# Four graph layers on one core: bias additions on GpSimd, one spread load, and a schedule found anew

## The chip, the cores and the metric

The kernel runs on one core of a Trainium2 chip. A core has five engines that work side by side, each on its own list of instructions in its own fixed order: TensorE (PE, matrix products and transposes), VectorE (DVE), ScalarE (ACT), GpSimd (POOL) and SyncE (SP, which here only issues transfers). Transfers run on 16 DMA engines that all queues share. The metric is the device time of one execution in microseconds (us), lower is better. Before the change it is 3014.25 us, the median of three runs between 3012.17 and 3017.27.

## The reference

Thirty-two graphs of 512 nodes with 256 features each go through four layers. Each layer ends in `x = layernorm(x + layer(x))`. All data is float32.

```
layer 0:  h = (1+eps)*x + adj@x ;  relu(h@W1 + b1)@W2 + b2
layer 1:  h = x@W per head (4 heads) ; e = leaky_relu(e_dst[i] + e_src[j])
          masked where adj <= 0.5 ; softmax over j ; attn@h + bias
layer 2:  q,k,v of 8 heads ; softmax(q.k/sqrt(32) + log(adj + 1e-6)) @ v ; @Wo.T + bo
layer 3:  softmax(mask(((x@W) @ x.T) * adj)) @ x
```

Three of the layers add a bias row of 256 numbers to every node: `b2`, `bias` and `bo`.

## The kernel before, in words

A graph lies in SBUF as 128 partitions by four chunks of nodes. One graph is a few hundred steps, each with an engine, an estimated duration, the steps that it needs, and the buffers that it takes and frees. `graph(g)` (line 556) declares these steps for each of the 32 graphs, `prepare()` those that load and transpose weights. Nothing is emitted yet. `Plan.order` (line 135) then walks through all steps as a list scheduler: among the steps that could start within `ahead` of the earliest one it takes that with the earliest due time, and so writes the one order in which every engine will work. Steps of up to six graphs are interleaved in that order, so that while one graph is in layer 0 another is in layer 2 or 3. `Plan.run` at the end of `fast_path` is called with the period, the other parameters, and fourteen pairs of a random seed and a distance that shift due times: the result of a search by annealing. What the planner believes of durations and of landing times decides the order; on the chip each instruction simply waits, in that order, until what it needs is there.

The planner also keeps stocks of buffers: `B` (8 KB per partition, such as the attention weights of one head or one chunk), `C` (4 KB), `D` (2 KB strips), and `p`, the eight PSUM banks. A transfer is three steps: the issue on a queue's engine, a time on the modelled queue (`.q`), and a landing delay of 2.0 us, written in `transfer` (line 315).

The parts around the change:

- **Biases.** `prepare` copies each bias row four times into a DRAM tile `biases`. `bias_steps(k)` (line 577) adds it to all of `x` (128x1024) by a GpSimd-issued transfer that accumulates in SBUF (line 583), after the last PE step that still needs the unbiased `x`: the product `h` in layer 0, the transposes `xt1` and `xt2` in layers 1 and 2. The result `xb{k}` is needed by the residual addition on VectorE.
- **Row R of layer 1.** For each head, `R` is a row of 512 factors that must stand on every partition. It is made as a column tile (with two further columns `xs`, sums of features), transposed on PE (`Rt`, line 853), copied by VectorE (`Re`), stored to DRAM as 18 rows in one transfer (`Rs`, line 863), and loaded back spread over the partitions in four transfers, one per head, into four `D` strips (`Rl0` to `Rl3`, line 872). A fifth transfer spreads the two `xs` rows (`hsb`, line 880), which VectorE multiplies with weights (`hsl`, line 888).
- **What uses R.** Sixteen ScalarE steps `z{h}{c}` (line 911) apply a relu to the spread row; VectorE multiplies the edge mask in (`zm`, line 922); PE forms the sums (`o1`, line 946). ScalarE also copies every PSUM result of PE, among them `he0` and `he1` (line 731), which the product `f` (line 747) needs.
- **Forms of the PE array.** Most products use the whole array. Scores `s` (line 1116) use four groups of 32 rows at once, `n` and `d1`, `d2` (lines 1174, 994, 1204) four groups of 32 columns, `o1` two groups of 64 columns. Products of the four or two groups run together.

Of the kernel before, what the change touches and what calls it, by code (L numbers as in the profile page):

```python
# [30 lines left out]
def row_bcast(ap, n):  # L31

    return bass.AP(tensor=ap.tensor, offset=ap.offset, ap=[[0, P], [1, n]])
# [13 lines left out]
class Plan:  # L47
# [30 lines left out]
    def step(self, name, eng, us, after=(), take=(), free=(), mode=""):  # L78


        def add(emit):
            steps = self.steps[-1]
            known = {**steps, **{f"^{n}": s for n, s in self.steps[0].items()}}
            assert name not in steps and all(a in known for a in after), (name, after)
            takes = []
            for b in take:
                kind, _, key = b.partition("=")
                key, _, rest = key.partition("/")
                takes.append((kind, key or kind, int(rest or 0)))
# [135 lines left out]
def fast_path(  # L225
# [65 lines left out]

    wT = {n: const.tile([P, DC, D], F32, name=f"w{n}T") for n in ("q", "k", "v", "o")}
    w3_sb = const.tile([P, DC, D], F32, name="w3_sb")
    biases = dram.tile([3, NC, D], F32, tag="biases", name="biases", bufs=1)


    def blk(i):
# [1 line left out]


    plan = Plan({
        "B": 11, "C": 12, "D": 19, "p": 8,

        "live": 6, "L0": 1, "L1": 2, "L2": 2, "L3": 1, "AT": 4, "zs": 7, "edge": 1, "tmp": 2,
    })
# [2 lines left out]
    def prev(name, i):  # L308

        return (f"{name}{i-1}",) if i else ()  # L310

    def row(name, n):
        return tuple(f"{name}{i}" for i in range(n))

    def transfer(name, us, after, queue="q1"):


        @step(f"{name}.q", queue, us, after)
        def _():
            pass  # L320

        @step(name, None, 2.0, (f"{name}.q",))
        def _():
            pass


    def prepare():
# [10 lines left out]
        def load(name, us, *transfers, take=(), little=False):  # L338


            @step(f"ld_{name}", "act" if little else "sp", 0.5 * len(transfers), take=take)
            def _():
                for transfer in transfers:
                    (nc.scalar if little else nc.sync).dma_start(*transfer())

            transfer(name, us, (f"ld_{name}",), "q3" if little else "q1")

        def rows(w):
            return w.rearrange("(c p) f -> p c f", p=P)
# [34 lines left out]
        load("w1", 2.5, lambda: (w1_sb, rows(w1)))  # L384
        load("w2", 2.5, lambda: (w2_sb, rows(w2)))

        def bias_rows(k, b):

            return lambda: (
                biases[k : k + 1], bass.AP(b.tensor, b.offset, [[0, 1], [0, NC], [1, D]])  # L390
            )

        load("bias", 0.6, *(bias_rows(k, b) for k, b in enumerate((b2, gbias, bo))), little=True)

        def vector(name, a):
            def transfer():
# [159 lines left out]
    def graph(g):  # L556
# [11 lines left out]
        def strip(key, shape, name):  # L568
            return sb.tile(shape, F32, tag=f"D{slot[key]}", name=f"{name}_{g}")
# [7 lines left out]
        def bias_steps(k, after):  # L577


            @step(f"xd{k}", "pool", 0.95, after + ("^bias",))  # L580
            def _():
                line = biases[k - 1 : k].rearrange("o c d -> o (c d)")
                nc.gpsimd.dma_start(  # L583
                    t["x"].rearrange("p c d -> p (c d)"), row_bcast(line, NC * D), accum_op=ALU.add
                )

            @step(f"xq{k}", "qa", 3.0, (f"xd{k}",))
            def _():
                pass

            @step(f"xb{k}", None, 2.5, (f"xq{k}",))
            def _():
                pass

        def norm_stats(n, c):
            nc.vector.bn_stats(t[f"st{n}"][:, c, :], t["xo" if n == 4 else "x"][:, c, :])  # L596
# [61 lines left out]
        for c in range(NC):  # L658

            @step(  # L660
                f"la{c}i", "sp", 0.45, (f"la{c-1}i",) if c else (),
                take=(f"D=A0{c}/5",) if c else ("live", "L0", "D=A00/8"),
            )
            def _(c=c):
                t[f"A{c}"] = strip(f"A0{c}", [P, N], f"A{c}")
                nc.sync.dma_start(t[f"A{c}"], adj[g].rearrange("(c p) m -> p c m", p=P)[:, c, :])

            transfer(f"la{c}", 1.0 if g == 0 else 2.0, (f"la{c}i",))

        @step("lxi", "sp", 0.45, (f"la{NC-1}i",), take=("C=x/2",))  # L670
        def _():
# [187 lines left out]

        @step("Rsi", "sp", 0.45, ("Re",))  # L860
        def _():
            t["Rdram"] = dram.tile([H1 * NC + DC, P], F32, tag="R_dram", name=f"R_dram_{g}")
            nc.sync.dma_start(t["Rdram"], t["Rr"])

        transfer("Rs", 0.2, ("Rsi",))

        for h in range(H1):

            @step(f"Rl{h}i", "sp", 0.45, ("Rs",) + ((f"Rl{h-1}i",) if h else ()), take=(f"D=R{h}/4",))
            def _(h=h):  # L870
                t[f"R{h}"] = strip(f"R{h}", [P, N], f"R_bc_{h}")
                nc.sync.dma_start(t[f"R{h}"], row_bcast(t["Rdram"][h * NC : (h + 1) * NC, :], N))

            transfer(f"Rl{h}", 0.8, (f"Rl{h}i",))


        @step("hsbi", "sp", 0.45, ("Rs",), take=("D=xsr/3",))
        def _():
            t["xsr"] = strip("xsr", [P, 2, D], "xs_row")
            nc.sync.dma_start(t["xsr"][:, 0, :], row_bcast(t["Rdram"][H1 * NC :, :], D))  # L880

        transfer("hsb", 0.4, ("hsbi",))

        @step("hsl", "dve", 0.7, ("hsb", "^weg"), free=("xsr",))
        def _():
# [18 lines left out]
        for h in range(H1):  # L904
            for c in range(NC):

                @step(f"z{h}{c}", "act", 0.7, (f"Rl{h}", "ST") + prev(f"z{h}", c), take=() if c else (f"B=z{h}",))
                def _(h=h, c=c):
                    if c == 0:
                        t[f"e{h}"] = big(f"z{h}", [P, NC, N], f"z1_{h}")  # L910
                    nc.scalar.activation(  # L911
                        t[f"e{h}"][:, c, :], t[f"R{h}"], AF.Relu,
                        bias=t["nT"][:, h, c : c + 1], scale=t["S"][:, h, c : c + 1],
                    )
# [12 lines left out]
        for h in range(H1):  # L927
            plan.free(f"R{h}", row(f"z{h}", NC))


        for hp in range(H1 // 2):
# [484 lines left out]
    for g in range(B):  # L1416
        graph(g)
    with tc.manual_schedule():
        plan.run([(33, 0.0, 6, 55.0, ((619770, 10.0), (518002, 10.0), (122525, 2.0), (401816, 5.0), (736052, 5.0), (898543, 5.0), (151957, 2.0), (89616, 2.0), (541939, 5.0), (120127, 10.0), (238703, 2.0), (316405, 2.0), (831071, 5.0), (164665, 2.0)), (0.7, 0.0, 0.0))])

# [470 lines left out]
```

## Time and profile before

| | value |
|---|---|
| median of three runs | 3014.25 us |
| the profiled execution: its time / its span | 3010.3 us / 3008.2 us |
| PE busy | 2938.5 us (98%) |
| VectorE, ScalarE, GpSimd busy | 2060.2, 1928.2, 626.8 us |
| transfers `x<-biases` | 96 of 512 KB, issued by GpSimd, 5.5 us from issue to landing |
| transfers `R_bc<-R_dram` | 128 of 256 KB, issued by SyncE |
| transfers `xs_row<-R_dram` | 32 of 128 KB, issued by SyncE |
| VectorE idle until `xs_row` landed | 209.2 us in 28 waits |
| ScalarE idle until `R_bc` landed | 181.6 us in 37 waits |

The span goes from the first to the last instruction of one profiled execution; its time includes what lies around it. Busy time of PE is the union of modelled instruction intervals, each of which goes on past the start of the next one, so 98% does not say that PE streams data 98% of the time. The start of one matmul to the start of the next is the better measure. A wait is put down to the releaser that came last.

### The profile page before, as it was taken

The numbers are of one execution on the slowest core, as the hardware profiler recorded it, in microseconds if no ns is written. First come the engines' busy times: TensorE is split into PE (matmuls) and PEld (weight loads), VectorE is DVE, ScalarE is ACT, GpSimd is POOL, SyncE is SP. The second block draws the span as 40 slices with busy tenths as digits, with TensorE's granted clock in tenths as the row PEclk, the third lists the DMA queues.
The fourth block names the chain that finished last, engine by engine and source line by source line (L and its number), as shares of the span: only waits on it lengthen the run. The fifth ranks groups of instructions, "written<-read, shape, count | busy, mean of one in ns | idle before, by whom it ended". The sixth has DMA issues, their size and how long they took to land.

```text
span 3008.2 us, 42752 instructions
## 1 busy us (share of the span) xinstructions
PE 2938.5 (98%) x15521; PEld 1687.7 (56%) x15521; DVE 2060.2 (68%) x4133; ACT 1928.2 (64%) x3818; POOL 626.8 (21%) x688
## 2 busy tenths in 40 slices
PE   8999999999999999999999999999999999999998
PEld 6546565565555565655656556555556565565544
DVE  3567767667667677676676766766767767667776
ACT  4666766666666667566676666665666766657664
POOL 1222212222122221222211222212222212222120
PEclk9999999999999999999999999999999999999999
DMA  6887787787787787877878777778778787786770
GB/s 175 179 173 171 166 188 161 167 177 156 173 176 168 164 173 166 191 159 160 182 149 192 163 167 175 163 167 186 164 165 168 163 191 157 166 179 143 163 171 15
DMA packets 180320, 498.89 MB, mean 166 GB/s; under 512 B 17980, under 2 KB 57736, under 8 KB 156296
## 3 DMA queue, kind: packets, MB, share of 16 engines
q0 software_dynamic: 77472, 346.06, 60.4%
q1 hardware_dynamic: 101648, 149.75, 15.5%
q8 instruction: 125, 2.05, 0.3%
q14 instruction: 91, 0.75, 0.1%
q10 hardware_dynamic: 984, 0.28, 0.0%
HBM read 183.25 MB, written 17.08 MB: 67 GB/s over the span
## 4 chain that ended last, share of the span: by engine, by line
PE 73%; DVE 10%; DMA 9%; ACT 5%; issue 2%; POOL 1%; SPq 0%; ACTq 0%; POOLq 0%; DVEq 0%
PE s L1317 8%; PE o_ps L1174 7%; PE s L1116 7%; PE y_ps L766 7%; PE o_ps L946 6%; DVE z L922 5%; PE o_ps L1371 5%; PE iT_ps L1303 4%; PE h1T_ps L747 4%; PE v_ps L815 4%; PE o2p_ps L1259 4%; ACT z L911 4%; PE v_ps L1097 4%; DMA xs_row<-R_dram 3%; DMA R_bc<-R_dram 3%; PE qT_ps L1079 2%
## 5 line engine op out<-in xcount | busy, mean ns | idle before, releaser
L1138 DVE SCALAR_TENSOR_TENSOR z<-AT,z 128x1024 f32<-128x1024 f32 x512 | 616.3, 1219 | 214.4 <-ACT z L1129 210.2
L1129 ACT ACTIVATE z<-s 128x512 f32<-128x512 f32 x1024 | 566.1, 602 | 126.9 <-PE s L1116 123.0
L911 ACT ACTIVATE z<-R_bc,nT,S 128x512 f32<-128x512 f32 x512 | 380.0, 809 | 181.7 <-DMA R_bc<-R_dram 181.6
L637 ACT ACTIVATE x<-x,shift,rstd 128x256 f32<-128x256 f32 x508 | 283.2, 592 | 127.9 <-DVE shift L627 127.8
L922 DVE SCALAR_TENSOR_TENSOR z<-z,T,edge 128x512 f32<-128x512 f32 x512 | 350.4, 746 | 10.7 <-ACT z L911 10.2
L1149 POOL DMA_DIRECT2D z<-z x186 | 165.9, 901 | 787.5 <-DVE z L1138 337.6
L1116 PE MATMUL s<-qT,kT 32*128 32x512 f32 x2048 | 313.3, 638 | 2.1 <-ACT qT L1085 2.1
L619 POOL TENSOR_TENSOR rstd<-ve,nhalf 128x4 f32<-128x4 f32 (+1 forms) x131 | 161.3, 1232 | 682.9 <-DVE ve L613 634.3
L974 POOL DMA_DIRECT2D z<-z x256 | 226.4, 953 | 300.1 <-DMA z<-z 183.4
L747 PE MATMUL h1T_ps<-hT,w_sb 128*128 128x512 f32 x512 | 243.0, 599 | 23.2 <-ACT hT L731 22.9
L946 PE MATMUL o_ps<-z,v 128*64 128x512 f32 x1024 | 244.9, 608 | 17.4 <-ACT z L1129 13.0
L1174 PE MATMUL o_ps<-z,v 128*32 128x512 f32 x2048 | 257.6, 600 | 3.8 <-DVE z L1138 3.8
L1223 DVE RECIPROCAL rdT<-rdT 128x256 f32<-128x256 f32 x128 | 219.2, 1735 | 54.0 <-ACT rdT L1216 53.8
L1371 PE MATMUL o_ps<-x,eT 128*128 128x256 f32 x1024 | 237.1, 380 | 0.0
L1317 PE MATMUL s<-xT,iT 128*128 128x512 f32 x512 | 236.4, 605 | 0.0
L766 PE MATMUL y_ps<-w_sb,h1T 128*128 128x256 f32 x1024 | 226.2, 379 | 0.0
L596 DVE BATCH_NORM_STATS2 st<-x 128x6 f32<-128x256 f32 x508 | 211.0, 415 | 8.3
L1116 PEld LDWEIGHTS s<-qT,kT 32*128 32x128 f32 x2048 | 103.6, 183 | 199.9 <-ACT z L1129 68.0
L724 PE MATMUL hT_ps<-AT,x 128*128 128x384 f32 (+2 forms) x768 | 208.8, 381 | 1.8 <-ACT AT L701 1.8
L766 PEld LDWEIGHTS y_ps<-w_sb,h1T 128*128 128x128 f32 x1024 | 194.3, 190 | 26.3
L583 POOL DMA_DIRECT2D x<-biases x96 | 86.0, 897 | 584.0 <-PE hT_ps L724 294.2
L1371 PEld LDWEIGHTS o_ps<-x,eT 128*128 128x128 f32 x1024 | 189.4, 190 | 31.5 <-ACT z L1129 0.8
(152 smaller groups left out, 4196.3 us busy)
## 6 DMA issues: line engine op xcount, KB each, us to landing
z<-z POOLq DMA_DIRECT2D x186, 1024.0 KB, 7.8
A<-in_adj_dram SPq DMA_DIRECT2D x256, 256.0 KB
z<-z POOLq DMA_DIRECT2D x128, 512.0 KB, 8.2
x<-biases POOLq DMA_DIRECT2D x96, 512.0 KB, 5.5
R_bc<-R_dram SPq DMA_DIRECT2D x128, 256.0 KB
z<-z POOLq DMA_DIRECT2D x128, 256.0 KB, 8.6
x<-in_x_dram SPq DMA_DIRECT2D x32, 512.0 KB
out_dram<-x SPq DMA_DIRECT2D x31, 512.0 KB
```

The lines of the kernel that those rows point to most:

```text
L637: nc.scalar.activation(xn, xn, AF.Identity, bias=t[f"shift{n}"][:, c : c + 1], scale=t[f"rstd{n}"][:, c : c + 1],)
L747: nc.tensor.matmul(ph, w1_sb[:, d, blk(f)], t["hT"][:, d, :], start=(d == 0), stop=(d == DC - 1))
L766: nc.tensor.matmul(py[:, j, :], t["h1T"][:, f, blk(2 * c2 + j)], w2_sb[:, f, :], start=(f == 0), stop=(f == HC - 1),)
L911: nc.scalar.activation(t[f"e{h}"][:, c, :], t[f"R{h}"], AF.Relu, bias=t["nT"][:, h, c : c + 1], scale=t["S"][:, h, c : c + 1],)
L922: nc.vector.scalar_tensor_tensor(z, z, t["T"][:, h, c : c + 1], t["edge"][:, c, :], op0=ALU.add, op1=ALU.mult)
L946: nc.tensor.matmul(po[j * F1 : (j + 1) * F1, :], t["v"][:, c, h * F1 : (h + 1) * F1], t[f"e{h}"][:, c, :], start=(c == 0), stop=(c == NC - 1),
L1116: nc.tensor.matmul(pk, t["k"][hs, o, blk(c)], t["q"][hs, o, :], start=True, stop=True)
L1129: nc.scalar.activation(t[f"E{k}"][:, j, :], t[f"ps{k}{j}"], AF.Exp, scale=QSCALE)
L1138: nc.vector.scalar_tensor_tensor(z, t["AT"][:, c, None, :].to_broadcast([P, 2, N]), ADJ_EPS, z, op0=ALU.add, op1=ALU.mult,)
L1174: nc.tensor.matmul(t[f"n{o}"][32 * j : 32 * j + 32, :], t["v2"][:, c, o * P + F2 * j : o * P + F2 * (j + 1)], t[f"E{k}"][:, j, :], start=( ...
L1317: nc.tensor.matmul(pt, t["iT"][:, d, blk(c)], t["xT3"][:, d, :], start=(d == 0), stop=(d == DC - 1),)
L1371: nc.tensor.matmul(py, t[f"eT{c}"][:, blk(m)], t["x"][:, m, :], start=(m == 0), stop=(m == NC - 1),)
```

## The change

Five edits.

1. The bias rows are loaded once, spread over all partitions, into a constant tile `bias_bc` (3 KB per partition), and each of the three additions per graph becomes one GpSimd `tensor_tensor` over 128x1024 elements. The DRAM tile and the accumulating transfers go.
2. Only the 16 rows of R are stored, and they come back in one transfer, 8 KB from DRAM to each partition, into one `B` buffer `R` instead of four strips. All sixteen `z` steps read that buffer. The two `xs` rows go through a store and a load of their own, and the order of issues on SyncE becomes: store R, store xs, load xs, load R.
3. In the plan, landing delays become 4.0 us by default, 5.0 us for the store and the load of R, and stay 2.0 us for the weights and the first graph's adjacency.
4. Stocks: 11 `B` buffers as before, 17 strips `D` instead of 19.
5. The planner's parameters and seeds are new, so the order of steps on every engine is new.

```diff
-    biases = dram.tile([3, NC, D], F32, tag="biases", name="biases", bufs=1)
+    bias_bc = const.tile([P, 3, D], F32, name="bias_bc")
...
-        "B": 11, "C": 12, "D": 19, "p": 8,
+        "B": 11, "C": 12, "D": 17, "p": 8,
...
-    def transfer(name, us, after, queue="q1"):
+    def transfer(name, us, after, queue="q1", land=4.0):
...
-        @step(name, None, 2.0, (f"{name}.q",))
+        @step(name, None, land, (f"{name}.q",))
...
-            @step(f"xd{k}", "pool", 0.95, after + ("^bias",))
+            @step(f"xb{k}", "pool", 2.5, after + ("^bias",))
             def _():
-                line = biases[k - 1 : k].rearrange("o c d -> o (c d)")
-                nc.gpsimd.dma_start(
-                    t["x"].rearrange("p c d -> p (c d)"), row_bcast(line, NC * D), accum_op=ALU.add
-                )
...
+                b = bias_bc[:, k - 1, None, :].to_broadcast([P, NC, D])
+                nc.gpsimd.tensor_tensor(t["x"], t["x"], b, ALU.add)
...
-            t["Rdram"] = dram.tile([H1 * NC + DC, P], F32, tag="R_dram", name=f"R_dram_{g}")
-            nc.sync.dma_start(t["Rdram"], t["Rr"])
+            t["Rdram"] = dram.tile([H1 * NC, P], F32, tag="R_dram", name=f"R_dram_{g}")
+            nc.sync.dma_start(t["Rdram"], t["Rr"][: H1 * NC, :])
...
-        for h in range(H1):
-
-            @step(f"Rl{h}i", "sp", 0.45, ("Rs",) + ((f"Rl{h-1}i",) if h else ()), take=(f"D=R{h}/4",))
-            def _(h=h):
-                t[f"R{h}"] = strip(f"R{h}", [P, N], f"R_bc_{h}")
-                nc.sync.dma_start(t[f"R{h}"], row_bcast(t["Rdram"][h * NC : (h + 1) * NC, :], N))
-
-            transfer(f"Rl{h}", 0.8, (f"Rl{h}i",))
+        transfer("Rs", 0.2, ("Rsi",), land=5.0)
+
+        @step("Rli", "sp", 0.45, ("Rs",), take=("B=R/3",))
+        def _():
+            t["Rbc"] = big("R", [P, H1, N], "R_bc")
+            nc.sync.dma_start(
+                t["Rbc"].rearrange("p h n -> p (h n)"), row_bcast(t["Rdram"], H1 * N)
+            )
+
+        transfer("Rl", 2.8, ("Rli",), land=5.0)
+
+        @step("xsi", "sp", 0.45, ("Re",))
+        def _():
+            t["xsdram"] = dram.tile([DC, P], F32, tag="xs_dram", name=f"xs_dram_{g}")
+            nc.sync.dma_start(t["xsdram"], t["Rr"][H1 * NC :, :])
...
-                        t[f"e{h}"][:, c, :], t[f"R{h}"], AF.Relu,
+                        t[f"e{h}"][:, c, :], t["Rbc"][:, h, :], AF.Relu,
...
-        plan.run([(33, 0.0, 6, 55.0, ((619770, 10.0), (518002, 10.0), (122525, 2.0), (401816, 5.0), (736052, 5.0), (898543, 5.0), (151957, 2.0), (89616, 2.0), (541939, 5.0), (120127, 10.0), (238703, 2.0), (316405, 2.0), (831071, 5.0), (164665, 2.0)), (0.7, 0.0, 0.0))])
+        plan.run([(28, 0.05, 6, 75.0, ((824592, 5.0), (893565, 10.0), (244737, 10.0), (911503, 5.0), (695937, 2.0), (23294, 5.0), (391254, 2.0), (207664, 2.0), (760101, 2.0), (339516, 5.0), (335230, 2.0), (34898, 2.0), (376325, 5.0), (379301, 2.0)), (0.6, 0.0, 0.1))])
```

More of the change, by code (lines that the diff above doesn't have):

```diff
@@ L344, in _ @@
                     (nc.scalar if little else nc.sync).dma_start(*transfer())
-            transfer(name, us, (f"ld_{name}",), "q3" if little else "q1")
+            transfer(name, us, (f"ld_{name}",), "q3" if little else "q1", 2.0)
         def rows(w):
@@ L385, in prepare, with bias_row @@
         load("w2", 2.5, lambda: (w2_sb, rows(w2)))
-        def bias_rows(k, b):
-            return lambda: (
-                biases[k : k + 1], bass.AP(b.tensor, b.offset, [[0, 1], [0, NC], [1, D]])
-            )
-        load("bias", 0.6, *(bias_rows(k, b) for k, b in enumerate((b2, gbias, bo))), little=True)
+        def bias_row(k, b):
+            return lambda: (bias_bc[:, k, :], row_bcast(b, D))
+        load("bias", 0.6, *(bias_row(k, b) for k, b in enumerate((b2, gbias, bo))), little=True)
         def vector(name, a):
@@ L577, in bias_steps @@
         def bias_steps(k, after):
-            @step(f"xd{k}", "pool", 0.95, after + ("^bias",))
+            @step(f"xb{k}", "pool", 2.5, after + ("^bias",))
             def _():
-                line = biases[k - 1 : k].rearrange("o c d -> o (c d)")
-                nc.gpsimd.dma_start(
-                    t["x"].rearrange("p c d -> p (c d)"), row_bcast(line, NC * D), accum_op=ALU.add
[L585 to L593, printed above, removed]
+                b = bias_bc[:, k - 1, None, :].to_broadcast([P, NC, D])
+                nc.gpsimd.tensor_tensor(t["x"], t["x"], b, ALU.add)
         def norm_stats(n, c):
@@ L666, in _ @@
                 nc.sync.dma_start(t[f"A{c}"], adj[g].rearrange("(c p) m -> p c m", p=P)[:, c, :])
-            transfer(f"la{c}", 1.0 if g == 0 else 2.0, (f"la{c}i",))
+            transfer(f"la{c}", 1.0 if g == 0 else 2.0, (f"la{c}i",), land=4.0 if g else 2.0)
         @step("lxi", "sp", 0.45, (f"la{NC-1}i",), take=("C=x/2",))
@@ L861, in _ @@
         def _():
-            t["Rdram"] = dram.tile([H1 * NC + DC, P], F32, tag="R_dram", name=f"R_dram_{g}")
-            nc.sync.dma_start(t["Rdram"], t["Rr"])
-        transfer("Rs", 0.2, ("Rsi",))
-        for h in range(H1):
-            @step(f"Rl{h}i", "sp", 0.45, ("Rs",) + ((f"Rl{h-1}i",) if h else ()), take=(f"D=R{h}/4",))
-            def _(h=h):
-                t[f"R{h}"] = strip(f"R{h}", [P, N], f"R_bc_{h}")
-                nc.sync.dma_start(t[f"R{h}"], row_bcast(t["Rdram"][h * NC : (h + 1) * NC, :], N))
-            transfer(f"Rl{h}", 0.8, (f"Rl{h}i",))
-        @step("hsbi", "sp", 0.45, ("Rs",), take=("D=xsr/3",))
+            t["Rdram"] = dram.tile([H1 * NC, P], F32, tag="R_dram", name=f"R_dram_{g}")
[12 more added lines that the diff above has]
+            nc.sync.dma_start(t["xsdram"], t["Rr"][H1 * NC :, :])
+        transfer("xs", 3.5, ("xsi",), "qx")
+        @step("hsbi", "sp", 0.45, ("xs",), take=("D=xsr/3",))
         def _():
             t["xsr"] = strip("xsr", [P, 2, D], "xs_row")
-            nc.sync.dma_start(t["xsr"][:, 0, :], row_bcast(t["Rdram"][H1 * NC :, :], D))
-        transfer("hsb", 0.4, ("hsbi",))
+            nc.sync.dma_start(t["xsr"][:, 0, :], row_bcast(t["xsdram"], D))
+        transfer("hsb", 2.0, ("hsbi",))
         @step("hsl", "dve", 0.7, ("hsb", "^weg"), free=("xsr",))
@@ L905, in graph @@
             for c in range(NC):
-                @step(f"z{h}{c}", "act", 0.7, (f"Rl{h}", "ST") + prev(f"z{h}", c), take=() if c else (f"B=z{h}",))
+                @step(f"z{h}{c}", "act", 0.7, ("Rl", "ST") + prev(f"z{h}", c), take=() if c else (f"B=z{h}",))
                 def _(h=h, c=c):
@@ L926, in graph @@
         plan.free("edge", tuple(f"zm{h}{k}" for h in range(H1) for k in range(2)))
-        for h in range(H1):
-            plan.free(f"R{h}", row(f"z{h}", NC))
+        plan.free("R", tuple(f"z{h}{NC-1}" for h in range(H1)))
         for hp in range(H1 // 2):
```

## The prediction

> **What bounds the kernel now.** I read the page first, then PE's waits, then PE's records in order of time, then ACT and DVE around PE's waits.
>
> ```profile
> span 3008.2 us, 42752 instructions
> ...
> PE 2938.5 (98%) x15521; PEld 1687.7 (56%) x15521; DVE 2060.2 (68%) x4133; ACT 1928.2 (64%) x3818; POOL 626.8 (21%) x688
> ...
> PEclk9999999999999999999999999999999999999999
> ```
>
> PE is nearly always in work and its clock is full; every other engine has a quarter or more of the span free. So only what lengthens or shortens PE's list can matter: its streaming (the matmuls are the same after), switching between array forms, and waits. The order of time shows the first two:
>
> ```profile
> 1880.47 1.98 PE L1303 MATMUL iT_ps<-xT,w_sb 128*128 128x512 f32 x4
> ...
> 1882.38 1.14 PE L1116 MATMUL s<-qT,kT 32*128 32x512 f32 x8
> ...
> 1883.45 1.98 PE L1303 MATMUL iT_ps<-xT,w_sb 128*128 128x512 f32 x4
> ...
> 1886.44 2.78 PE L1174 MATMUL o_ps<-z,v 128*32 128x512 f32 x24
> ...
> 1889.15 1.14 PE L1116 MATMUL s<-qT,kT 32*128 32x512 f32 x8
> ```
>
> Undisturbed, a 512-column matmul follows the last one after 0.429 us (the chain in order of time has 16 of `h1T` in 6.87), a 256-column one after 0.216 (32 of `y_ps` in 6.91); four `s` or `n` matmuls share one such slot, two `o1`. Above, four `i` matmuls take 1.91 us from start to next start, where 4 x 0.429 is 1.72: 0.19 for this stretch of one form. Eight `s` take 1.07 against 0.86: 0.21. Twenty-four `n` take 2.71 against 2.57: 0.14. Over all stretches without a wait the medians are: `s` 0.213, 32-column 0.138, 64-column 0.150, full array 0.198 (0.151 when transposes come first). In the built order I count 227, 198, 68 and 204 such stretches: about 124 us. Streaming at the pitches above is 2750 us. With 5.0 us ahead of the first matmul and 8.5 after the last one's start, 3008.2 - 13.5 - 2750 - 124 leaves about 121 us of waits on PE.
>
> ```profile
> PE h1T_ps L747 <- ACT hT L731: 22.9, 24, 2.2
> PE o_ps L946 <- ACT z L1129: 13.0, 15, 2.1
> PE AT_t L691 <- DMA A<-in_adj_dram: 6.3, 2, 5.0
> ```
>
> These are idle times beyond a matmul's modelled end; from start to start, the gaps over 0.3 us inside `f` make 26.5 us (23), inside `o1` 17.7 (21). The same place of most graphs explains them:
>
> ```profile
> 1920.62 1.52 ACT L911 ACTIVATE z<-R_bc,nT,S 128x512 f32<-128x512 f32 x2 [5.93 <-DMA R_bc<-R_dram]
> ...
> 1925.34 0.56 ACT L731 COPY hT<-hT_ps 128x512 f32<-128x512 f32 x1
> 1925.81 2.93 ACT L911 ACTIVATE z<-R_bc,nT,S 128x512 f32<-128x512 f32 x4
> 1928.64 0.57 ACT L731 COPY hT<-hT_ps 128x512 f32<-128x512 f32 x1
> ```
>
> ACT stands 5.93 us for `R_bc`, then has ten `z` ahead of the second `hT` copy, and `f` waits for that copy. DVE meanwhile stood 7.33 us for `xs_row`. ACT is still behind when the two first `s` steps of a graph come back to back:
>
> ```profile
> 1933.75 2.98 PE L1116 MATMUL s<-qT,kT 32*128 32x512 f32 x16
> 1936.66 1.94 PE L946 MATMUL o_ps<-z,v 128*64 128x512 f32 x8
> ```
>
> Two steps need 1.93 (4 slots and 0.21) and take 2.91: 0.98 more, as PSUM banks are not yet emptied. The trace has this 28 times, 27.4 us. Together 26.5 + 17.7 + 27.4 = 71.6 us of waits hang on two transfers that land later than the plan's 2.0 us; the other 49 us are the first and last graphs and short ones.
>
> **What the Trainium skill says.** TensorEngine Tiling (Array Packing), "Key Properties": a change of tiling mode drains the array; the trace agrees (0.14 to 0.21 us per stretch). GPSIMD Engine Reference, 3.1: a `tensor_tensor` add of 2048 fp32 takes 4497 ns, twice DVE's; I estimate half, 2.25 us, for 1024. No 1024-wide GpSimd operation is in this trace. SBUF — State Buffer, "SBUF: two separate sides", on the shared port pair: a GpSimd operation and a DVE operation with two SBUF inputs, or in a 2-port mode, exclude each other for the whole instruction. Here 60 of the `zm` overlap a GpSimd `rstd` and are no longer (748 against 747 ns), but `rstd` has 4 columns, so it tells little.
>
> **The change part by part.**
>
> *Array forms.* The new order has 250 `s`, 200 32-column, 74 64-column and 301 full stretches: 53.3 + 27.6 + 11.1 + 53.9 = 146 us at the durations above. PE pays +21.5 us for certain; no other work hides it.
>
> *R and xs.* SP issues two stores and two loads where it issued one and five. In the trace a store took 4.7 us from issue to the next issue (1910.49 to 1915.23), spread loads 5.4 to 9.2. In the new order `hsl` stands on DVE behind the last `yt` of the graph before; from `Rt` to there PE has a product `h` (3.49), two `n`, two `s`, three `f` and smaller steps, some 13 us; xs needs 0.6 + 0.7 + 4.7 + 0.5 + 5.5, about 12. The first `z` stand on ACT behind the second exponential of layer 3, some 23 us after `Rt`; R, issued last, needs about 6.5 plus 8 for 1 MB (accumulates of 1 MB land in 7.8), 14.5. Both `hT` copies now stand behind score exponentials alone, with 2.6 us of `n`, `n`, `s` between `h` and `f` where the copy needs about 1. Two `s` steps in a row remain in 6 places, not 29. So of the three waits I take all 71.6 us away. If R lands over 8 us later than this, for want of a `B` buffer, they return.
>
> *Bias additions.* 96 issues of 0.897 us (86 us of POOL) go, 96 additions of about 2.25 (216) come: POOL goes from 21 to about 25% and is no bound. Removed transfers (50 of 346 MB on that queue) free nothing on PE's path: PE waits 0.4 us in all for accumulates. Behind an addition on POOL stand one or two `rstd` (layer norms that PE reads over 10 us later) or an accumulate that has over 10 us until `d2`. What can cost is DVE, if it is shut out. The addition of layer 2, after `xt2`, comes where DVE has `zm`, but `o1` is 6 us off; that of layer 0, after `h`, precedes an `m` whose `n` comes 10 us later. That of layer 1, after `xt1`, is tight: four edge comparisons and the first `m` follow on DVE, and `n` has about 0.6 us to spare. A free addition costs 0; two blocked operations, 2.25 + 1.25 of the `rstd` behind it, cost 3.5 - 0.6 = 2.9 us per graph, 93 in all. I take 0.2 us per graph.
>
> *New tight places.* Windows of 0.1 to 0.7 us are left at the bank of `s` after `AT`, at `t` after `i`, and at `y` after `f`; I take 0.4 us per graph. With the additions: 0.6 x 32 = 19 us, an estimate; 0 at best, 93 and more at worst. Head and tail are reordered; I take no difference, give or take 8. Fewer strips and three larger bias loads at the start are hidden: the first addition comes after the first `h`, the first residual later still.
>
> Sum: 3008.2 + 21.5 - 71.6 + 19 = 2977 us span, 31 less. The profiled execution took 3010.3, the median is 3014.25, so the median after is about 2983.
>
> **Rivals.** *The waits move.* The plan's new windows are narrow, and R in one piece waits for a `B` buffer and lands whole. For it: no buffer was added for R, and `AT` of three graphs, four `z` and up to four chunks of layer 2's weights fill the stock. Against: 8 us of room. If half of the 71.6 us come back, -36 + 21.5 + 19 is +5: 3019, about no change; with three quarters 3037, with a quarter 3001. *DVE is shut out.* For it: the lock as stated, and 16 `m` and 16 `zm` per graph with two SBUF inputs. Against: DVE is 32% idle and only one place is tight. At 93 us in place of 19: 2983 + 74 = 3057; from 1.6 us per graph (52 us) it is slower than before. *Nothing but the order matters:* the landings change which engine waits, but PE's waits keep their sum; then +21.5, 3036.
>
> **How the numbers follow.** A measurement of this kernel tells some 0.2% (6 us) from no change. The forecast, 2965 to 3000, has 0.62; waits that move 0.18 (a third each faster, same, slower); DVE shut out 0.10 and order alone 0.05, slower; better than 2965, with no new waits, 0.05. Faster: 0.62 + 0.06 + 0.05 = 0.73; same 0.06; slower 0.06 + 0.10 + 0.05 = 0.21. The range, 2960 to 3030, leaves out the longer ends of the slower cases (some 0.14) and the largest gains (0.03); the forecast's own range stands above.
>
> **What would show it.** Right: no `R_bc` and `xs_row` waits above some 20 us on ACT and DVE, `f <- hT` near nothing, 0.98 us gone from the second `s`, PE's stretches 825, busy PE down. Wrong: `n` waiting for `z` of DVE with `m` or comparisons longer than 1.22 and 0.42 us beside a GpSimd addition; additions well over 2.3 us; SP waiting long before the load of R.

## The result, and the profile after

The changed kernel takes 2973.29 us, the median of four runs (2972.07 to 2974.01), beside 3015.76 us (3012.17 to 3021.0) for the kernel before in the same comparison: a ratio of 0.9857, with a 95% interval from 0.984 to 0.9874. The profiled execution has a span of 2972.2 us where before had 3008.2, so 36.0 us went.

The head of its page, and the shares of the chain that ended last:

```profile
span 2972.2 us, 42591 instructions
...
PE 2929.2 (99%) x15521; PEld 1662.6 (56%) x15521; DVE 2127.1 (72%) x4133; ACT 1918.8 (65%) x3818; POOL 776.0 (26%) x688
...
PE 91%; DVE 3%; ACT 3%; DMA 2%; issue 1%; POOL 0%; POOLq 0%; ACTq 0%
```

The chain now runs through PE for 91% of the span; before it was 73%, with 10% on DVE and 9% on transfers. VectorE is busy 67 us longer than before, which will matter below. The costliest waits of PE, and from the page's groups `zm` and the reader of R (busy time, mean ns, then idle time before it and its releaser):

```profile
PE o_ps L940 <- DVE z L917: 8.7, 2, 8.1
PE AT_t L679 <- DMA A<-in_adj_dram: 7.7, 2, 4.7
PE AT_t L679 <- DVE rd L1010: 4.4, 24, 0.2
```

```profile
L917 DVE SCALAR_TENSOR_TENSOR z<-z,T,edge 128x512 f32<-128x512 f32 x512 | 412.4, 857 | 10.6 <-ACT z L906 10.1
L906 ACT ACTIVATE z<-R_bc,nT,S 128x512 f32<-128x512 f32 x512 | 382.9, 807 | 8.9 <-DMA R_bc<-R_dram 5.2
```

`f <- hT` (22.9 us before) and `o1 <- z` of layer 2 (13.0) are gone from PE's waits. ScalarE's wait for `R_bc` fell from 181.6 us to 5.2, VectorE's for `xs_row` from 209.2 us to none. What PE still waits for is an 8.1 us stand at 107 us, in the first graphs, and many short stands at the bank of `AT`.

PE's time can be split as the prediction split it, now stretch by stretch: in each stretch of one array form, the time beyond its streaming up to the median of its kind is the cost of the form, and what is more is a wait.

| profiled execution | forms | waits | first and last (5.0 + 8.5 before) |
|---|---|---|---|
| before | 123.9 us in 695 stretches | 114.3 us | 13.5 us |
| after | 144.8 us in 823 stretches | 54.8 us | 13.0 us |

Forms +20.9, waits -59.5, the ends -0.4: -39.0 together, where the span fell by 36.0. The other 3 us fall outside the split, which takes one pitch for all streaming; the work that is streamed is the same. The counts of stretches leave out two that the prediction's counts have.

### The profile page after: what moved, and what is told of

It is laid out like the page before. It is cut to its first block, busy times and chain, and to the rows that moved or that the text cites. A ratio compares the mean times of both kernels' runs of the same rounds, so it can differ in the third digit from the quotient of the medians.

```text
span 2972.2 us, 42591 instructions
## 1 busy us (share of the span) xinstructions
PE 2929.2 (99%) x15521; PEld 1662.6 (56%) x15521; DVE 2127.1 (72%) x4133; ACT 1918.8 (65%) x3818; POOL 776.0 (26%) x688
## 4 chain that ended last, share of the span: by engine, by line
PE 91%; DVE 3%; ACT 3%; DMA 2%; issue 1%; POOL 0%; POOLq 0%; ACTq 0%
PE s L1110 9%; PE h1T_ps L735 8%; PE o_ps L1168 8%; PE o_ps L940 7%; PE hT_ps L712 7%; PE o_ps L1365 7%; PE s L1311 7%; PE y_ps L754 7%; PE v_ps L803 4%; PE iT_ps L1297 4%; PE o2p_ps L1253 4%; PE v_ps L1091 4%; PE qT_ps L1073 3%; PE kT_ps L1073 3%; PE d_ps L1198 2%; PE eT_t L1350 2%
## 5 line engine op out<-in xcount | busy, mean ns | idle before, releaser
L917 DVE SCALAR_TENSOR_TENSOR z<-z,T,edge 128x512 f32<-128x512 f32 x512 | 412.4, 857 | 10.6 <-ACT z L906 10.1
L581 POOL TENSOR_TENSOR x<-x,bias_bc 128x1024 f32<-128x1024 f32 x96 | 238.9, 2489 | 382.0 <-PE hT_ps L712 160.3
L625 ACT ACTIVATE x<-x,shift,rstd 128x256 f32<-128x256 f32 x508 | 289.6, 599 | 19.6 <-DVE shift L615 19.6
L1110 PE MATMUL s<-qT,kT 32*128 32x512 f32 x2048 | 294.9, 638 | 1.1 <-DVE y L1023 0.6
L607 POOL TENSOR_TENSOR rstd<-ve,nhalf 128x4 f32<-128x4 f32 (+1 forms) x131 | 144.5, 1146 | 545.3 <-DVE ve L601 530.0
L1168 PE MATMUL o_ps<-z,v 128*32 128x512 f32 x2048 | 264.2, 601 | 0.3 <-DVE z L1132 0.3
L940 PE MATMUL o_ps<-z,v 128*64 128x512 f32 x1024 | 237.8, 603 | 8.7 <-DVE z L917 8.7
L1341 ACT ACTIVATE z<-z,nmax 128x512 f32<-128x512 f32 x128 | 92.4, 722 | 193.2 <-DVE nmax L1333 191.7
```

The lines of the kernel that those rows point to most:

```text
L917: nc.vector.scalar_tensor_tensor(z, z, t["T"][:, h, c : c + 1], t["edge"][:, c, :], op0=ALU.add, op1=ALU.mult)
L940: nc.tensor.matmul(po[j * F1 : (j + 1) * F1, :], t["v"][:, c, h * F1 : (h + 1) * F1], t[f"e{h}"][:, c, :], start=(c == 0), stop=(c == NC - 1),
L1110: nc.tensor.matmul(pk, t["k"][hs, o, blk(c)], t["q"][hs, o, :], start=True, stop=True)
L1168: nc.tensor.matmul(t[f"n{o}"][32 * j : 32 * j + 32, :], t["v2"][:, c, o * P + F2 * j : o * P + F2 * (j + 1)], t[f"E{k}"][:, j, :], start=( ...
```

## Experiments

**Which late transfer was PE paying for?** Three kernels keep the kernel before and its order on every engine, and let a reader of a late row read a constant row instead. The transfers still run. Layer 1's values are then not the reference's. In `b_const_R` the first form of `z` on ScalarE reads a row of `w1`, in `b_const_xs` VectorE's `hsl` reads a row of `w2`, and `b_const_both` has both:

```diff
-                        t[f"e{h}"][:, c, :], t[f"R{h}"], AF.Relu,
+                        t[f"e{h}"][:, c, :], w1_sb[:, 0, :], AF.Relu,
...
-                    t["xsr"][:, 1, :], t["xsr"][:, 0, :], wgT[:, o, :], TINY, 0.0,
+                    t["xsr"][:, 1, :], w2_sb[:, 0, :], wgT[:, o, :], TINY, 0.0,
```

> The kernel before, its order unchanged, but the z steps on ACT read a weight tile instead of the spread R, and hsl on DVE a weight row instead of xs, so neither waits for a transfer (all transfers are still made; the values of layer 1 are not the reference's). Theory (the late landings cause PE's waits in f, in the second s and in o1): these 71.6 us go, nothing else changes: about 2944 us, faster than the changed kernel, as the new order's 21.5 us of form changes are not paid. Rival (the order alone makes the waits; they move): 2995 to 3015.

> As b_const_both, but only the z steps on ACT are freed of their transfer; DVE still waits for xs. Theory: the 54 us of f and of the second s go, o1's 17.7 us stay in part: 2950 to 2962. Rival (DVE's wait for xs is what PE feels): within 15 us of the kernel before.

> As b_const_both, but only hsl on DVE is freed; ACT still waits for R. Theory: at most o1's 17.7 us go: 2997 to 3015. Rival (DVE's wait is what PE feels): 50 us or more faster.

| | median, us | ratio to before, 95% interval | waits on PE, us |
|---|---|---|---|
| before (in that comparison) | 3015.16 | | 114.3 |
| `b_const_R` | 3011.63 | 0.999 (0.9978 to 1.0001) | 110.0 |
| `b_const_xs` | 3001.71 | 0.9955 (0.9935 to 0.9974) | 102.2 |
| `b_const_both` | 2919.55 | 0.9686 (0.9669 to 0.9704) | 23.6 |

The theory for `b_const_R` failed and its rival held; `b_const_both` came out 24 us under its theory, `b_const_xs` within its own. Freeing ScalarE alone gave 3.5 us, freeing VectorE alone 13.5, and both together 95.6. The costliest wait of PE in `b_const_R`:

```profile
PE o_ps L946 <- ACT z L1129: 63.2, 28, 2.3
```

in `b_const_xs`:

```profile
PE h1T_ps L747 <- ACT hT L731: 25.5, 26, 2.2
```

and in `b_const_both`, where each is down to single stands:

```profile
PE AT_t L691 <- DMA A<-in_adj_dram: 7.4, 2, 4.8
PE o_ps L1174 <- DVE z L1138: 5.7, 2, 3.6
```

So two waits stood side by side. With R in time, ScalarE was ahead again and `f` and the second `s` lost nothing, but VectorE still stood for `xs_row` with the `zm` behind it. PE then lost at `o1` what it had lost at `f` and `s` before: by pitch, `o1` takes 74.4 us more than in `b_const_both`, and `f` 0.1. With xs in time it was the other way round: `f` 33.4, `s` 26.6 and `o1` 12.1 us more. A cause can carry nearly the whole price and yet be worth nothing alone. Stretch by stretch the pair cost 114.3 - 23.6 = 90.7 us: `f` 30.9, `s` 27.0, `o1` 25.2, `v` of layer 2 4.8, and the rest in ones.

**The bias additions alone, in the old order.** `b_bias_pool` is the kernel before with the first edit and nothing else; the order on all engines is the old one. For want of space one spread row serves all three additions, so the values differ from the reference.

```diff
-                line = biases[k - 1 : k].rearrange("o c d -> o (c d)")
-                nc.gpsimd.dma_start(
-                    t["x"].rearrange("p c d -> p (c d)"), row_bcast(line, NC * D), accum_op=ALU.add
-                )
+                b = bias_bc[:, 0, None, :].to_broadcast([P, NC, D])
+                nc.gpsimd.tensor_tensor(t["x"], t["x"], b, ALU.add)
```

> The kernel before, its order and its R transfers unchanged, with the first edit alone: the bias additions on GpSimd (for want of space one spread bias row serves all three additions, so two layers add another row than the reference). Theory (additions and removed transfers both lie beside PE's path): within 8 us of the kernel before. Rival (DVE shut out): 40 us or more slower. Rival (fewer transfers let R land earlier): 15 us or more faster.

Measured: 3103.82 us (3101.76 to 3105.78), a ratio of 1.0297 (1.028 to 1.0314). The edit by itself makes the kernel 89 us slower, and the expectation of at most 8 us failed. VectorE in one graph, in order of time (start, duration, then the instruction):

```profile
1033.04 0.43 DVE L884 CUSTOM_DVE_ANT_0 xs_row<-xs_row,wgT 128x256 f32<-128x256 f32 x1 [7.33 <-DMA xs_row<-R_dram]
...
1033.86 8.82 DVE L918 SCALAR_TENSOR_TENSOR z<-z,T,edge 128x512 f32<-128x512 f32 x10
```

and GpSimd and PE in the same graph:

```profile
1033.92 2.91 POOL L581 TENSOR_TENSOR x<-x,bias_bc 128x1024 f32<-128x1024 f32 x1 [8.88 <-PE hT_ps L720]
...
1050.67 2.38 PE L942 MATMUL o_ps<-z,v 128*64 128x512 f32 x6 [2.31 <-ACT z L1125]
```

An addition of one graph begins 0.06 us after the first `zm`, when VectorE had stood 7.33 us for `xs_row` and had sixteen `zm` to make up. One of them is held until the addition ends: up to 2.95 us where 0.75 is usual, so that ten take 8.82 us, where two more take 1.38 undisturbed a little later, thus about 6.8. PE's `o1`, which waits for these `zm` (the page names an exponential that was long done), stands 2.31 us more. Summed over the trace, 19 `zm` are held for 40.4 us, 9 `hsl` for 19.1, and 29 residual additions `x<-x,y` for 40.3; PE loses 62 us more at `o1` than before and 25 at the `s` after `f`, while the 31 us at `f` fall to 3; the rest is spread. The lock is as large as the prediction's rival had it (93 us), but at another place.

`b_bias_none` parts the two sides of that edit: the kernel before without any bias addition (`x` lacks its biases), so with the relief of the transfer engines and without the lock.

```diff
-                nc.gpsimd.dma_start(
-                    t["x"].rearrange("p c d -> p (c d)"), row_bcast(line, NC * D), accum_op=ALU.add
-                )
+                pass
```

> The kernel before, its order kept, with the 96 bias additions left out altogether (x lacks its biases): neither the accumulating transfers nor GpSimd's additions. It takes the first edit's relief of the transfer engines without its lock on VectorE. Theory (with the additions on GpSimd VectorE waited 208 us for xs_row as before and ScalarE 148 for R_bc instead of 182; so the transfers were not what made xs late): 2995 to 3017, likeliest 3008, with the xs_row wait near 200 us. Rival (the bias transfers stood ahead of R's store as in i_pool_dma, so both rows now come some 3 us earlier): 2940 to 2985, with the waits for xs_row and R_bc halved.

Measured: 2991.93 us (2990.15 to 2994.11), a ratio of 0.992 (0.9899 to 0.9941), 3 us below the theory's bound and 7 above the rival's. R is read 8.1 us after its store instead of 9.9 (medians), nearly all of it in the load (3.3 instead of 5.1); the wait for `R_bc` falls from 181.6 us to 131.3, that for `xs_row` only from 209.2 to 192.1. So the relief is worth 22 us here, and the additions themselves cost 3103.82 - 2991.93 = 112 us. The trace shows VectorE's instructions held for 111 us, but the two are not one for one. The record of the granted clock in `b_bias_pool` has 22 stretches at half speed, 78.5 us in all between the first 20 us and PE's last matmul, where `b_bias_none` has 5 with 20.5 us; most come behind a stand of PE (the last section shows one). By an estimate from these records, half of the stretches without PE's idle time in them, the slow clock costs 38 us in the one and 9 in the other. So some 29 of the 112 us are matmuls that ran slower after a stand, and some 83 are stands and other delays: on this estimate PE pays about three quarters of the lock directly.

**The same edit in the new order.** `a_bias_dma` is the changed kernel with the accumulating transfers back in the places of the additions:

```diff
-                b = bias_bc[:, k - 1, None, :].to_broadcast([P, NC, D])
-                nc.gpsimd.tensor_tensor(t["x"], t["x"], b, ALU.add)
+                line = biases[k - 1 : k].rearrange("o c d -> o (c d)")
+                nc.gpsimd.dma_start(
+                    t["x"].rearrange("p c d -> p (c d)"), row_bcast(line, NC * D), accum_op=ALU.add
+                )
```

> The changed kernel with its bias additions put back to the accumulating transfers of the kernel before, issued from the same 96 places of GpSimd's order (order of every engine as in the changed kernel). In the changed kernel the first reader of x comes 11 us or more after every addition, so a landing of some 9 us delays nobody, and 91 us of lengthened VectorE instructions go away. Theory (in the new order the first edit is hidden, and what remains of the lock is worth a few us): 2960 to 2978, likeliest 2967. Rival (the 24 MB a graph set free on the transfer engines is what lets R and xs land in time): 2990 or more, with waits for R_bc or xs_row back on ScalarE or VectorE.

Measured: 2970.88 us (2968.39 to 2972.45), a ratio of 0.9845 (0.9829 to 0.9862), which does not differ from the changed kernel's 0.9857; this is within the theory. (The transfers move 1.5 MB a graph, 50 MB in all, and not the 24 MB a graph that the expectation names.) VectorE is busy 2037.0 us instead of 2127.1. So in this order it makes no difference that can be measured whether additions or transfers add the biases; no run of this order leaves both out, so what either costs by itself is not shown. Yet the lock is there in the changed kernel too: 91 us of held instructions, 59.3 of them in 29 `zm`. VectorE and PE around one of them:

```profile
1081.77 3.49 DVE L917 SCALAR_TENSOR_TENSOR z<-z,T,edge 128x512 f32<-128x512 f32 x2
```

```profile
1086.85 3.60 PE L1073 MATMUL qT_ps<-xT,wqT 128*128 128x512 f32 x8
1090.29 3.60 PE L1073 MATMUL kT_ps<-xT,wkT 128*128 128x512 f32 x8
...
1095.54 0.65 PE L940 MATMUL o_ps<-z,v 128*64 128x512 f32 x2
```

Two `zm` take 3.49 us where 1.4 is usual, but PE has `w`, `q`, `k` and `w` again ahead of `o1`, some 10 us.

`a_bias_twice` asks how much of that room is left. Each addition is executed twice in a row (so `x` has each bias twice).

> The changed kernel with each of the 96 bias additions executed twice in a row (x receives each bias twice, so its values differ); it doubles the time in which GpSimd holds the shared port, 227 us more on GpSimd and by the first additions' 91 us some 90 to 200 us more on VectorE. Theory (the new order gives VectorE room at these places): 2978 to 3005, likeliest 2990. Rival (the room is used up by the first addition): 3040 or more, each further addition costing TensorE the 0.9 us it cost in the old order, or all 2.2.

Measured: 3016.67 us (3014.89 to 3021.02), a ratio of 1.0006 (0.9997 to 1.0015): 43 us above the changed kernel, between the two expectations. VectorE's held time grows from 91 to 214 us, and PE pays 43 of the 123 more, 0.45 us per addition. From start to start, `d1`, which reads `z` after its accumulating transfers, takes 18 us more, `n` 7, `o1` and `s` 5 each. The room of the new order is worth about one addition; the second is paid for by a third.

**R in one transfer or in four.** `a_R_four` is the changed kernel with the spread of R issued as four transfers into the same buffer.

```diff
-            nc.sync.dma_start(
-                t["Rbc"].rearrange("p h n -> p (h n)"), row_bcast(t["Rdram"], H1 * N)
-            )
+            for h in range(H1):
+                nc.sync.dma_start(t["Rbc"][:, h, :], row_bcast(t["Rdram"][h * NC : (h + 1) * NC, :], N))
```

> The changed kernel with the one spread of R issued as four transfers, one per head, from the same place of SP's order into the same large buffer. Theory (the later landings in the plan are what removes the waits, and three more issues of about 0.5 us each on SP fall into slack): within 6 us of 2973. Rival (the single transfer in long runs is what brings R in time): 2985 or more, with ScalarE waiting for R_bc by over 50 us in all.

Measured: 2983.47 us (2981.78 to 2983.97), a ratio of 0.9889 (0.9872 to 0.9905), 10 us above the changed kernel; ScalarE waits 19.4 us for `R_bc` in 6 places, where the changed kernel has 5.2 in 2. Neither expectation had it. The loss lies in two places out of 32. SyncE and ScalarE at one of them:

```profile
2522.94 3.26 SPq L859 DMA_DIRECT2D R_bc<-R_dram  x4
```

```profile
2534.47 0.81 ACT L905 ACTIVATE z<-R_bc,nT,S 128x512 f32<-128x512 f32 x1 [6.43 <-DMA R_bc<-R_dram]
...
2539.00 0.56 ACT L1354 COPY eT<-eT_t 128x512 f32<-128x512 f32 x1
```

The load is issued late there, since SyncE waits for the buffer of R. The four issues take 3.26 us, R is there 11 us after the first, and a copy `eT` of layer 3 stands behind two `z` on ScalarE; PE's `w` waits 5.2 us for it. Everywhere else the load has room, and its form is worth nothing. So, but for these two graphs, it is the order and not the form of the load that brings R in time. Which part of the plan made that order, the longer landings, the stocks or the new seeds, no run here separates: none searches anew with the old landings.

**What the new order costs.** `a_const_both` makes in the changed kernel the same two substitutions as `b_const_both`; layer 1's values are not the reference's.

> The changed kernel with the two readers of late transfers freed: ScalarE's first form of z reads a constant row of w1 in place of R_bc, and VectorE's hsl a constant row of w2 in place of xs_row (layer 1's values are not the reference's; the transfers still run). Against the same edit in the old order (2920) it shows what the new order itself costs when no transfer is late. Theory (the new order pays 21.5 us in changes of TensorE's form, and some 20 in short waits and the lock): 2955 to 2970, so about 40 us above the old order. Rival (the new order costs nothing, and what separates 2973 from 2920 are transfers still late): 2915 to 2935.

Measured: 2971.83 us (2971.42 to 2973.1), a ratio of 0.9852 (0.9836 to 0.9869), 2 us above the theory's range. So no more than some 2 us of these two landings are left in the changed kernel, and with both readers freed the new order, its additions on GpSimd included, is 52 us slower than the old one (2919.55). PE's split says where: forms 144.7 against 123.9 us, +20.9; waits 51.9 against 23.6, +28.3. Of the waits, 18 us lie in stretches that begin with `AT`. Eight of them are the one stand at 107 us; the rest are the transposes of `AT`, which the new order puts in one row between `s` and `n`. PE of the changed kernel in order of time:

```profile
1035.17 1.14 PE L1110 MATMUL s<-qT,kT 32*128 32x512 f32 x8
1036.24 0.66 PE L679 MATMUL AT_t<-ident,A 128*128 128x128 f32 x4
...
1038.06 0.66 PE L679 MATMUL AT_t<-ident,A 128*128 128x128 f32 x4 [0.18 <-DVE rd L1010]
1038.65 1.06 PE L1168 MATMUL o_ps<-z,v 128*32 128x512 f32 x8
```

The group is a stretch of its own, with two changes of form, and in it the last four transposes wait for a bank. In the old order the transposes stood by eights among full-array work (between `v` of layer 1 and `u`, and between `xt` and `w`, 28 times each), and had neither.

**An order with fewer changes of form.** If forms and short waits are what the new order pays, a search that knows the price of forms should find a better one. `i_pool` is the changed kernel with the measured stretch costs in the planner's table, and parameters and seeds searched anew under it, with 28 pairs of seed and distance instead of fourteen; all else is the changed kernel's.

```diff
     CHANGE = {
-        "": {"": 0.0, "row": 0.13, "c32": 0.1, "c64": 0.1},
-        "row": {"": 0.17, "row": 0.1, "c32": 0.2, "c64": 0.2},
-        "c32": {"": 0.12, "row": 0.12, "c32": 0.0, "c64": 0.12},
-        "c64": {"": 0.12, "row": 0.12, "c32": 0.12, "c64": 0.0},
+        "": {"": 0.0, "row": 0.213, "c32": 0.138, "c64": 0.15},
+        "row": {"": 0.198, "row": 0.1, "c32": 0.138, "c64": 0.15},
+        "c32": {"": 0.198, "row": 0.213, "c32": 0.0, "c64": 0.15},
+        "c64": {"": 0.198, "row": 0.213, "c32": 0.138, "c64": 0.0},
     }
...
-        plan.run([(28, 0.05, 6, 75.0, ((824592, 5.0), (893565, 10.0), (244737, 10.0), (911503, 5.0), (695937, 2.0), (23294, 5.0), (391254, 2.0), (207664, 2.0), (760101, 2.0), (339516, 5.0), (335230, 2.0), (34898, 2.0), (376325, 5.0), (379301, 2.0)), (0.6, 0.0, 0.1))])
+        plan.run([(27, 0.1, 6, 50.0, ((797991, 10.0), (751936, 10.0), (868113, 10.0), (334447, 5.0), (700230, 5.0), (433706, 10.0), (364421, 5.0), (510494, 5.0), (722768, 5.0), (968199, 1.0), (638697, 2.0), (264782, 2.0), (608952, 2.0), (298837, 1.0), (746864, 2.0), (605474, 1.0), (79930, 2.0), (30011, 2.0), (41419, 2.0), (611640, 2.0), (928293, 2.0), (838694, 1.0), (181267, 1.0), (540670, 1.0), (85769, 1.0), (78043, 1.0), (71481, 1.0), (747318, 1.0)), (0.6, 0.0, 0.0))])
```

> The changed kernel with two things different: the planner's table of costs for changing TensorE's array form holds the measured costs of a stretch (0.213 us into row groups, 0.138 into 32-column, 0.150 into 64-column groups, 0.198 back to the full array), and the planner's parameters and seeds are a new search under that table. The work, the landing delays and the buffers are the changed kernel's. With that table the planner gives this order 540 changes of form and an end at 2905 us; the changed kernel's own order has 824 changes and would end at 2968 under it, and took 2973. Theory (what the new order of the changed kernel paid was forms and short waits, not the additions or the landings): 2900 to 2930, likeliest 2912. Rival (an order without room at the additions pays VectorE's lock again, up to 89 us as in the old order): 2950 or more, with lengthened zm or x additions ahead of TensorE's waits.

Measured: 2926.76 us (2925.62 to 2927.62), a ratio of 0.9705 (0.9688 to 0.9721): 46.5 us below the changed kernel and within the expectation, if at its upper end. PE's split: forms 93.5 us in 539 stretches, 51 less than the changed kernel; waits 55.7, about the same. So fewer changes of form account for the gain. What made the search find them is less certain: the table and the longer list of seeds changed together, and no run has the one without the other. PE in order of time:

```profile
1439.82 3.62 PE L1365 MATMUL o_ps<-x,eT 128*128 128x256 f32 x16
1443.37 3.65 PE L940 MATMUL o_ps<-z,v 128*64 128x512 f32 x16
```

Longer pieces of one form: `w` stands in sixteens 59 times and `n` in forties 26 times, where the changed kernel has `w` in eights 64 times and `n` in eights 132 times. What PE now waits for most is the exponential of layer 3, which is late in 28 graphs:

```profile
PE eT_t L1350 <- ACT z L1341: 15.2, 28, 1.2
```

**Two of the same kind with accumulating transfers.** `i_dma` has a search of its own under the same table, with the bias additions as accumulating transfers (as in the kernel before, but 5.0 us of landing in the plan) and 19 strips. `i_pool_dma` keeps the order of `i_pool` and puts the transfers in the places of the additions; its diff is that of `a_bias_dma`.

> The same table and a search of its own, with the bias additions as accumulating transfers (5.0 us of landing in the plan, 3.0 on the queue) and 19 strips. The planner gives 582 changes of form and an end at 2911. Theory: 2900 to 2935, likeliest 2915, thus the same as with additions on GpSimd within 10 us. Rival (additions on GpSimd cost TensorE something in a tight order): this one is faster by 15 us or more.

> The kernel of i_pool with the bias additions put back to accumulating transfers in the same 96 places; order of every engine as in i_pool, whose first readers of x come 12 us or more after an addition. It tells whether i_dma was slower for the 50 MB more on the transfer engines, or for its own plan (there SyncE stood 200 us for the buffer of R). Theory (the plan: the buffer of R was one that an accumulating transfer of z still held): 2915 to 2937, likeliest 2925, ScalarE waiting for R_bc under 25 us. Rival (in an order with fewer changes of form the relief of the transfer engines is needed): 2945 or more, with R_bc waits of 50 us or more.

Measured: `i_dma` 2969.72 us (2961.83 to 2973.11), a ratio of 0.9844 (0.9822 to 0.9866); `i_pool_dma` 3017.54 (3011.81 to 3026.35), a ratio of 1.0008 (0.9999 to 1.0017). Both missed their theory, the first by 35 us and the second by 80, where the rival of the second (2945 or more, 50 us of waits for `R_bc`) came true. In `i_dma` part of the loss is its plan's: SyncE stands 199.6 us in 25 waits for the buffer of R, until an accumulating transfer of `z` has left it. I had taken that for the whole of it, and `i_pool_dma` shows that it need not be. There SyncE has the buffer as soon as in `i_pool`, but R is late all the same. SyncE around one R in `i_pool`:

```profile
1409.04 0.32 SPq L851 DMA_DIRECT2D R_dram<-R_rows  x1
...
1413.75 0.34 SPq L875 DMA_DIRECT2D xs_row<-xs_dram  x1
1414.32 0.78 SPq L858 DMA_DIRECT2D R_bc<-R_dram  x1
```

and the same in `i_pool_dma`, with GpSimd's issue of a bias transfer shortly before it:

```profile
1446.98 0.33 SPq L855 DMA_DIRECT2D R_dram<-R_rows  x1
...
1454.45 0.34 SPq L879 DMA_DIRECT2D xs_row<-xs_dram  x1
1455.08 0.60 SPq L862 DMA_DIRECT2D R_bc<-R_dram  x1
```

```profile
1441.69 0.87 POOL L583 DMA_DIRECT2D x<-biases  x1 [5.04 <-PE hT_ps L716]
```

The 512 KB of that addition, 5 us old, are ahead of the two small stores (8 KB of R and 1 KB of xs) on the same transfer engines, and the first load, that of xs, is issued 7.5 us after the store of R instead of 4.7. Over all graphs the median from the store of R to the load of R is 8.3 us instead of 5.0, and to the first `z` 22.3 instead of 18.6. In the six graphs that have no bias transfer in the 6 us ahead of the store, the first load comes no later than in `i_pool`. ScalarE waits 77.0 us in 29 places for `R_bc`, where `i_pool` has 5.0 in 4, and hands it on to PE:

```profile
PE kT_ps L1077 <- ACT xT L1062: 73.7, 26, 4.5
```

The stands are not all of it. From start to start, PE loses 108 us more inside `k` than in `i_pool`, which is some 34 us beyond the stands: the matmuls after them run slower for a while (last section). The `u` that waited in `i_pool` gives 19 back.

In the changed kernel the first `z` comes 26.0 us after the store by the median, in `a_bias_dma` too, and the load of R itself waits for a buffer until 13.5 us after it; there 3 us more on the store are not seen.

## Why the prediction was right, and where it was not

The forecast was 2983 us, 31 less than before; measured were 2973.29 and 42. Of its terms, one gain came out 19 us larger and one loss 12 us larger, so errors of opposite sign make the sum better than its parts. Its sum was made against the profiled execution, 2977 us of span, and the span is 2972.2; the other 5 us come from carrying the profile before, which lies 4 us under its median, to the median. Term by term:

| term | predicted, us | measured, us | from |
|---|---|---|---|
| forms | +21.5 | +20.9 | stretches before and after |
| waits on R and xs that go | -71.6 | -90.7 | before and `b_const_both` |
| new waits with the additions | +19 | +31.2 | `b_const_both` and after |
| of these, the additions | +6 | about 2, against the transfers | `a_bias_dma` and after |

- **Array forms: right**, in number and price; the medians per stretch are the same after.
- **R and xs: the mechanism right, the size too small by 19 us.** `f` (26.5 predicted, 30.9 measured) and the second `s` (27.4, 27.0) were well read. `o1` was not: only gaps over 0.3 us were counted, 17.7 us, where the two late rows cost 25.2 there, and 4.8 more at layer 2's `v`, which the prediction put with the "short ones". By the estimate of half speed used above, some 8 of the 90.7 us are matmuls that ran slower after a stand (10 us before, 2 in `b_const_both`), which the prediction does not have. It also took the 71.6 us as a sum over two transfers. `b_const_R` and `b_const_xs` show that they are not: 3.5 and 13.5 us apart, 95.6 together.
- **The landings of the new order: right in the outcome, with less room than it says.** R is read 26 us after its store (predicted some 23 after `Rt`), and `a_const_both` finds under 2 us left of such waits. But SyncE does stand for the buffer of R, which the prediction names as a sign of being wrong:

```profile
SPq L858 <- DVE y L1023: 200.8, 24, 17.7
```

  Counted from `Rt`, the load is issued after 14.1 us by the median, where the prediction took about 6.5: nearly all of its 8 us of room is used. ScalarE still waits only 5.2 us, since the first `z` comes 26.6 us after `Rt`, 12.5 after the load. With the load in four pieces two graphs lose 10 us (`a_R_four`), and in `i_dma`, where SyncE stands for this buffer too, ScalarE waits 86.5 us in 29 places, in part by the mechanism that the rival names.
- **New tight places: too small by 12 us.** They were put at 0.4 us per graph, at the bank of `s` after `AT` among others. It is `AT` itself that waits for its bank, some 10 us in all, and the start, put at nothing give or take 8, lost 8.3.
- **Bias additions: right in the sum, wrong in the place.** The prediction expected the lock at layer 1's comparisons and the first `m`. The trace has 14.2 us held in comparisons and 59.3 in `zm`, beside the addition of layer 2, which it had passed over as harmless; it is, since `o1` is far. The rival was as large as it said: 89 us in the old order (`b_bias_pool`), 43 in the new one when doubled.
- **"Removed transfers free nothing on PE's path": right for this order only.** With 12.5 us between the load of R and its reader nothing shows (`a_bias_dma`); in the order of `i_pool` the same transfers in place of the additions cost 91 us. In the kernel before they were worth 22 (`b_bias_none`).

## What to carry to other kernels

Two waits that stand side by side are worth nothing one by one, so a suspect is tried both alone and with its neighbour before it is cleared. An edit in a scheduled kernel has no price of its own: the same additions cost 89 us on balance in one order, nothing in a second, and save 91 in a third, according to the room that the order leaves at their places; so state an edit's price with the slack that hides it. A late input can cost more than the time for which PE stands, since PE ran at half speed for a few us after many of the longer stands. And it is worth trying to give a planner the measured price of what it can trade: with forms at their measured cost, and twice as many seeds, the search found an order 46 us faster with the same work.

## What was not expected of the hardware

- **What an addition on GpSimd holds on VectorE.** The Trainium skill, SBUF — State Buffer, "SBUF: two separate sides", has the shared port pair held for a whole instruction against a VectorE operation with two SBUF inputs or in a 2-port mode. The traces agree for two inputs: beside a 128x1024 addition (2.37 us, from 2.34) `zm` takes up to 2.90 us instead of 0.74, an `m` 3.38 instead of 1.22, `x<-x,y` in `b_bias_pool` 1.77 by the median instead of 0.39. But for the length of the hold the measurement decides: 60 `zm` beside a 128x4 `rstd` of GpSimd, some 1.2 us long and with two inputs in SBUF, are no longer than others (748 against 747 ns in the profile before). Operations with one SBUF input and one PSUM input (`x<-x,o2p_ps`, 26 beside an addition, at most 0.68 us) and the statistics of a layer norm (52, at most 0.43) are not held. But `edge<-AT`, a comparison with one input, is (up to 2.13 instead of 0.42), and so is `ve`, with four columns (up to 2.25 instead of 0.16); whether these are the page's 2-port case no run here tells.
- **A small store waits behind a large transfer of another queue.** From the issue of the 8 KB store of R to the issue of the load that needs it are 5.0 us by the median in `i_pool`, and 8.3 in `i_pool_dma`, where in 26 graphs a 512 KB accumulate was issued 5.3 to 5.7 us before it.
- **After a stand PE ran at half speed for a few us.** PE in `i_pool_dma`:

```profile
825.92 4.34 PE L1077 MATMUL kT_ps<-xT,wkT 128*128 128x512 f32 x6 [3.75 <-ACT xT L1062]
830.05 1.27 PE L1354 MATMUL eT_t<-ident,z 128*128 128x128 f32 x8
```

  Six products take 4.13 us where six times 0.429 are 2.57; the last three start 0.85 us apart. The granted clock is 0.50 from 827.5 to 830.4 us and 1.00 from 831.2 to 834.7. The record has 18 such stretches in this run, most of them 3.4 us long and some 6.8, 78.5 us in all between the first 20 us and PE's last matmul, and 2 with 10.2 us in `i_pool`; in `b_bias_pool` 19 of 22 follow within 9 us of a gap of 2.7 us or more. Not every stand is followed by one: `b_const_R` has 31 gaps over 1.5 us and 6 such stretches. What length of stand brings one no run here tells.
